# Attention scores in eight array tiles of one head each, with the previous half group's weighing put into the right halves of the same four banks

## The chip, the cores and the metric

The kernel runs on one core of one Trainium2 chip. The time is that of the device for one execution, in microseconds (us). TensorE (PE) does matrix products into PSUM, VectorE (DVE) and ScalarE (ACT) read PSUM and do elementwise work, GpSimd (POOL) does elementwise work in SBUF only, SyncE (SP) issues the transfers. PSUM has eight banks of 128 partitions by 512 fp32 values.

## The reference

Four residual layers follow one another on 128 graphs of 64 nodes with 256 features: `x = x + layer(relu(layernorm(x)))`. Layers 0 and 1 are attention layers with eight heads of 32 features. Layer 0 masks by the adjacency; layer 1 adds the logarithm of the adjacency to the scores. The part that the change touches, cut to what matters:

```python
q = split_heads(x @ Wq + bq)          # layer 1 has no q, k, v biases
k = split_heads(x @ Wk + bk)
v = split_heads(x @ Wv + bv)
scores = jnp.einsum('bhqd,bhkd->bhqk', q, k) / sqrt(HD)      # HD = 32
scores = jnp.where(adj > 0, scores, NEG)                     # layer 0
scores = scores + jnp.log(adjacency + 1e-06)                 # layer 1
attn = softmax(scores, axis=-1)
out = jnp.einsum('bhqk,bhkd->bhqd', attn, v)                 # called weighing below
return out @ Wo + bo
```

Layer 2 is a gated recurrent unit over five rounds of `A.T @ (h @ weight[l])`; its gates make up most of the matrix work. Layer 3 is a gated pair of graph convolutions.

## The kernel before, in words

**Tiling and stages.** Two graphs make a pair of 128 rows, four pairs make a group, and there are 16 groups. Attention works on half a group at a time (two pairs), so there are 16 x 2 layers x 2 halves = 64 calls of `attend`, the half groups of this text. Everything is fp32; each fp32 matmul that isn't a transpose stands twice in the profile's records, as two passes.

**Order of the work.** The instructions are not issued in program order. Every operation is handed to a planner (class `Plan`) with its engine, an assumed cost, its reads and writes, and a due time. The stages lie on strands: the attention of group g+1 (`front`), the recurrent rounds of group g (`gru`) and layer 3 of an earlier group (`back`) overlap. The planner walks through time and writes one fixed order for each engine's queue. On the chip every engine then works through its queue in that order and waits where a semaphore is not yet there. The constants at the head (`AHEAD`, `FRONT_LAST`, `STEP_SPAN`, `LOCK` and so on) shift due times. `CHANGE` holds the costs that the planner assumes for a switch between the modes of the array: whole (`WIDE`), tiles of 64 rows by 64 columns (`T64`), tiles of 64 by 32 (`T32`), and transposes (`TURN`).

**PSUM.** Four of the eight banks (`gate`, tag "g") are kept for the gates of the recurrent unit: tiles `gb`, `gc`, `nb`, `nc`, line 994. The other four (`bank`, tag "a") serve everything else: layernorm transposes `lnT` (L547), `qkvb` and `qkvc` (L711), scores `s`, weighing `o`, output projection `y` (L879), aggregation `agg` (L1034), transposes `hT`, and layer 3 (`l3b`, `l3c`, `hom`).

**Attention of one half group.** `by_seven` (58 of the 64) or `plainly` (6) make q, k and v. `spread` (L653, ACT) then copies k twice into `k_exp`: one copy keeps the even heads and zeroes the odd ones, the other the reverse. With it one score matmul covers 64 rows of q (two heads) and yields both heads side by side: 16 matmuls of 64 x 64 weights and 128 moving columns (L775), on four tiles of the array, into two banks. ACT takes the exponential of each bank (L797, two instructions of 512 columns), and POOL multiplies by the mask (L799). Weighing is done one half group later: `weigh` (L843, and L851 for the sums of the exponentials by a column of ones) in tiles of 64 by 32 into two further banks, where the left half of a bank holds outputs and the right half sums. `divide` on DVE turns the sums (L861), takes the reciprocal (L862), turns it back (L863) and multiplies (L865) into `oT`. Four matmuls of `y` and the residual addition (L882) end it. Weighing of the last half group and scores of this one are two separate operations of the planner, so that other work may stand between them.

A second copy of the whole network (`lean` false) stands behind a branch that is not taken here.

Of the kernel before, what the change touches and what calls it, by code (L numbers as in the profile page):

```python
# [55 lines left out]
AHEAD = 2.0  # L56
# [4 lines left out]
FRONT_LAST = 0.15  # L61
# [3 lines left out]
BACK_SPAN = 0.7  # L65
STEP = 0.0
STEP_LAST = -0.1
STEP_SPAN = 0.5
LOCK = 0.3
BACK_END = 0.1  # L70
ENTRY = 0.05
FIRST = -1.2
# [6 lines left out]
WEIGH = (655, 950)  # L79
MASK_UP = 2.0 ** 32  # L80
# [208 lines left out]
def network(ctx: ExitStack, tc: tile.TileContext, a: dict, out: bass.AP, flag):  # L289
# [343 lines left out]
    def attend(layer, xt, half, bias, bias_at, name, plain):  # L633
# [7 lines left out]
        k_exp = new("kexp", [P, 2, 2, HALF], 1, f"kexp_{name}")  # L641
# [17 lines left out]
        def plainly():  # L659

            (tq, jq), (tk, jk), (tv, jv) = of_first[layer]

            def dense(ps, t, j, hold):
                for o in range(2):
                    for kc in range(2):
                        pe(mm(256), lambda o=o, kc=kc: nc.tensor.matmul(
                            ps[:, o * HALF : (o + 1) * HALF], t[:, j, kc, o * P : (o + 1) * P], hT[:, kc, :],
                            start=kc == 0, stop=kc == 1), [(t, j), hT], [ps], holds=[hold])

            pq, pk, pv = bank(f"q_{name}"), bank(f"k_{name}"), bank(f"v_{name}")  # L670
            split = lambda ps: ps.tile.rearrange("p (c g t) -> p c g t", c=2, g=2)
            dense(pq, tq, jq, qk)
            if biased:
                for c in range(2):
                    vec(dve(256, 1), lambda c=c: nc.vector.tensor_scalar(
                        qk[:, c, :, 0, :], split(pq)[:, c], cols[:, c : c + 1], None, op0=ALU.add),
                        [pq, cols], [(qk, (c, 0))])
            else:
                vec(dve(512), lambda: nc.vector.tensor_copy(qk[:, :, :, 0, :], split(pq)), [pq], [(qk, (0, 0))])
            dense(pk, tk, jk, k_exp)  # L680
            spread(lambda c: split(pk)[:, c], [pk])
            for gp in range(2):
                for kc in range(2):
                    pe(mm(256), lambda gp=gp, kc=kc: nc.tensor.matmul(
                        pv[:, gp * D : (gp + 1) * D], side(kc, gp)(), tv[:, jv, kc, :],
                        start=kc == 0, stop=kc == 1), [(tv, jv), hT], [pv], holds=[v])
            sca(act(512), lambda: nc.scalar.activation(
                v.tile, pv.tile.rearrange("p (g f) -> p g f", g=2), AF.Copy), [pv], [v])

        def by_seven():  # L690
# [27 lines left out]
            def keep(bk, nm, c):  # L718

                t = new("cp", [P, 4, P], 5, f"{nm}_{name}")  # L720
                if biased:
                    sca(act(128, 1), lambda: nc.scalar.activation(
                        t[:, 0, :], bk[:, :P], AF.Identity, bias=cols[:, c : c + 1]), [bk, cols], [(t, 0)])
                    sca(act(256), lambda: nc.scalar.activation(t[:, 1:3, :], part(bk, 1), AF.Copy), [bk], [(t, 1)])
                else:
                    sca(act(384), lambda: nc.scalar.activation(t[:, :3, :], part(bk), AF.Copy), [bk], [(t, 0), (t, 1)])
                return t

            def total(bk, t, c, gp):
                vec(dve(256), lambda: nc.vector.tensor_tensor(  # L730
                    qk[:, c, gp], part(bk, 0, 2), t[:, :2, :], op=ALU.add), [bk, (t, 0), (t, 1)], [(qk, (c, gp))])
# [16 lines left out]
            if biased:  # L748
                for j in range(2):
                    sca(act(128, 1 - j), lambda j=j: nc.scalar.activation(  # L750
                        qk[:, 1, 0, j, :], pb[:, j * P : (j + 1) * P], AF.Copy if j else AF.Identity,
                        **({} if j else dict(bias=cols[:, 1:2]))), [pb, cols], [(qk, (1, 0, j))])
            else:
                sca(act(256), lambda: nc.scalar.activation(qk[:, 1, 0], part(pb, 0, 2), AF.Copy), [pb], [(qk, (1, 0))])
            sca(act(128), lambda: nc.scalar.activation(v[:, 0, P:], pb[:, 2 * P : 3 * P], AF.Copy), [pb], [(v, (1, 0))])
            spread(lambda c: qk[:, c, :, 1, :], [qk])
# [6 lines left out]
        pss = [bank(f"s_{name}_{i}") for i in range(2)]  # L763

        def scores():
            for outer in range(2):
                for c in range(2):
                    for inner in range(2):
                        for rh in range(2):
                            i, gp = (inner, outer) if lean else (outer, inner)  # L770
# [3 lines left out]
                            to, at = (i, gp) if lean else (gp, i)  # L774
                            nc.tensor.matmul(ps[to * NODES : (to + 1) * NODES, 2 * c : 2 * c + 2, at, :],  # L775
# [5 lines left out]
        if waiting:  # L781
# [12 lines left out]
        for i in range(2):  # L794
            ps, e = pss[i], es[i]
            if lean:
                sca(act(512, 0.5), lambda ps=ps, e=e: nc.scalar.activation(  # L797
                    e.tile, ps.tile.rearrange("p (h k) -> p h k", h=4), AF.Exp, scale=scale), [ps], [e])
# [3 lines left out]
                continue  # L802
# [30 lines left out]
        po = [bank(f"o_{name}_{i}") for i in range(2)]  # L833

        def weigh():
            for gp in range(2):
                s = slice(gp * NODES, (gp + 1) * NODES)
                for c in range(2):
                    for q in range(4):
                        for i in range(2):  # L840
                            rows, h = slice(i * NODES, (i + 1) * NODES), 4 * c + q
                            o = po[i][:, :D].rearrange("p (c t) -> p c t", c=2)
# [5 lines left out]
                for q in range(4):  # L848
                    for i in range(2):
                        rows = slice(i * NODES, (i + 1) * NODES)  # L850
                        nc.tensor.matmul(po[i][q * HD : (q + 1) * HD, D:], ones[rows, :],  # L851
# [3 lines left out]
        oT = new("oT", [P, 2, 2, P], 1, f"oT_{name}")  # L855

        def divide(i):
            zt = new("zt", [P, D], 2, f"zt_{name}_{i}")
            rz = new("rz", [P, HEADS], 2, f"rz_{name}_{i}")
            blocks = lambda t: t.tile.rearrange("p (b t) -> p b t", t=32)  # L860
            vec(dve(256), lambda: nc.vector.transpose(zt.tile, po[i][:, D:]), [po[i]], [zt])  # L861
            vec(109, lambda: nc.vector.reciprocal(rz[:, :, None], blocks(zt)[:, :, :1]), [zt], [rz])  # L862
            vec(dve(256), lambda: nc.vector.transpose(  # L863
                blocks(zt), rz[:, :, None].to_broadcast([P, HEADS, 32])), [rz], [zt])
            vec(dve(256), lambda: nc.vector.scalar_tensor_tensor(  # L865
                oT[:, i].rearrange("p c t -> p (c t)"), zt.tile, WEIGH_UP, po[i][:, :D],
                op0=ALU.mult, op1=ALU.mult), [po[i], zt], [(oT, i)])

        def finish():
            for i in range(2):  # L870
                if lean:
                    divide(i)
                    continue
                vec(dve(256), lambda i=i: nc.vector.tensor_copy(
                    oT[:, i], po[i][:, :D].rearrange("p (c t) -> p c t", c=2)), [po[i]], [(oT, i)])
            py = bank(f"y_{name}")
            for i in range(2):
# [7 lines left out]
                [py, (xt, pp), (xt, pp + 1)], [(xt, pp), (xt, pp + 1)])  # L885

        waiting.append((xt, weigh, [v, *aTs], po, oT, finish))

    def flush(xt):

        if not waiting or waiting[-1][0] is not xt:
            return
        _, weigh, reads, po, oT, finish = waiting.pop()
        pe(WEIGH[lean], weigh, reads, po, holds=[oT], mode=T32)
        finish()
# [638 lines left out]
```

## Time and profile before

| | |
|---|---|
| time, median of 3 (lowest to highest) | 2507.91 us (2506.99 to 2508.75) |
| span of the profiled execution | 2505.0 us |
| PE busy | 2483.1 us, 99% |
| DVE busy | 1875.7 us, 75% |
| ACT busy | 1304.8 us, 52% |
| POOL busy | 889.4 us, 36% |
| score matmuls (L775), records | 2048, 69.7 us busy |
| weighing matmuls (L843 and L851), records | 4096 and 1024, 71.8 and 49.8 us busy |
| copies into k_exp (L653) | 192, 98.2 and 10.2 us busy |
| exponentials (L797) | 128, 69.5 us busy |

Busy time of matmuls on array tiles overlaps, so a burst's real cost is read from the timeline: from its first start to the start of what follows. The rows of a group give the mean duration of one instruction and, behind the bar, how long its engine was idle just before it.

### The profile page before, as it was taken

The numbers are of one execution on the slowest core, as the hardware profiler recorded it, in microseconds if no ns is written. First come the engines' busy times: TensorE is split into PE (matmuls) and PEld (weight loads), VectorE is DVE, ScalarE is ACT, GpSimd is POOL, SyncE is SP. The second block draws the span as 40 slices with busy tenths as digits, with TensorE's granted clock in tenths as the row PEclk, the third lists the DMA queues.
The fourth block names the chain that finished last, engine by engine and source line by source line (L and its number), as shares of the span: only waits on it lengthen the run. The fifth ranks groups of instructions, "written<-read, shape, count | busy, mean of one in ns | idle before, by whom it ended". The sixth has DMA issues, their size and how long they took to land.

```text
span 2505.0 us, 58714 instructions
## 1 busy us (share of the span) xinstructions
PE 2483.1 (99%) x24057; PEld 2131.6 (85%) x24057; DVE 1875.7 (75%) x4396; ACT 1304.8 (52%) x2654; POOL 889.4 (36%) x894
## 2 busy tenths in 40 slices
PE   9999999999999999999999999999999999999997
PEld 7888888888888888888888888888888888888885
DVE  6666777777777777787778777777777777877667
ACT  3455454555555455555554555555554555555544
POOL 6633433333333332423334333333333424333221
PEclk9999999999999999999999999999999999999999
DMA  6411212112222121222113122122221212211120
GB/s 207 171 61 64 94 62 88 65 53 84 72 80 72 62 74 65 82 69 80 59 62 102 50 88 83 52 81 72 80 68 59 76 66 80 72 46 71 49 71 19
DMA packets 78266, 188.60 MB, mean 75 GB/s; under 512 B 14802, under 2 KB 66852, under 8 KB 67108
## 3 DMA queue, kind: packets, MB, share of 16 engines
q1 hardware_dynamic: 77872, 184.71, 21.6%
q8 instruction: 192, 3.15, 0.5%
q14 instruction: 86, 0.70, 0.1%
q10 hardware_dynamic: 116, 0.04, 0.0%
HBM read 166.70 MB, written 18.02 MB: 74 GB/s over the span
## 4 chain that ended last, share of the span: by engine, by line
PE 97%; DVE 2%; ACT 0%; issue 0%; POOL 0%; DMA 0%; DVEq 0%; ACTq 0%; POOLq 0%
PE gb L994 22%; PE gc L994 17%; PE nb L994 11%; PE nc L994 8%; PE qkvb L711 6%; PE qkvc L711 5%; PE y L879 4%; PE agg L1034 3%; PE l3b L1339 3%; PE s L775 2%; PE l3c L1339 2%; PE lnT L547 2%; PE hT L547 2%; PE o L843 2%; PE o L851 1%; PE gv L930 1%
## 5 line engine op out<-in xcount | busy, mean ns | idle before, releaser
L1103 POOL TENSOR_TENSOR sn<-h,sn 128x512 f32<-128x512 f32 x158 | 205.5, 1304 | 664.3 <-ACT sn L1101 664.3
L994 PE MATMUL gb<-Ta,gv 128*128 128x256 f32 x960 | 248.1, 381 | 0.0
L994 PE MATMUL gb<-Th,w_hh 128*128 128x256 f32 x960 | 247.9, 381 | 0.0
L963 POOL TENSOR_TENSOR Th<-h 128x256 f32<-128x256 f32 x160 | 120.4, 772 | 333.6 <-PE nb L994 230.6
L533 POOL TENSOR_TENSOR rstd<-pw,few 128x2 f32<-128x2 f32 x128 | 94.9, 741 | 382.6 <-DVE pw L532 380.6
L799 POOL TENSOR_TENSOR e<-e,mask 128x512 f32<-128x512 f32 x128 | 176.2, 1396 | 105.9 <-ACT e L797 105.9
L994 PEld LDWEIGHTS gb<-Th,w_hh 128*128 128x128 f32 x960 | 177.5, 190 | 23.4 <-issue 1.9
L994 PEld LDWEIGHTS gb<-Ta,gv 128*128 128x128 f32 x960 | 177.1, 191 | 23.4 <-issue 2.1
L1101 ACT ACTIVATE sn<-sn,b_n 128x512 f32<-128x512 f32 x158 | 113.4, 722 | 132.9 <-DVE sn L1099 132.5
L994 PE MATMUL gc<-h,w_hh 128*128 128x256 f32 x640 | 167.4, 384 | 0.1
L994 PE MATMUL gc<-agg,gv 128*128 128x256 f32 x640 | 164.6, 380 | 0.0
L1105 DVE SCALAR_TENSOR_TENSOR sn<-sg,sn 128x512 f32<-128x512 f32 x158 | 107.4, 686 | 62.9 <-POOL sn L1103 62.6
L1086 ACT ACTIVATE sg<-sg,b_rz 128x512 f32<-128x512 f32 x158 | 106.6, 715 | 90.3 <-DVE sg L1066 90.2
L963 POOL TENSOR_TENSOR Th<-h,Th 128x256 f32<-128x256 f32 x160 | 144.8, 905 | 8.6 <-DVE h L1107 2.9
L1097 DVE SCALAR_TENSOR_TENSOR sn<-sg,sn 128x512 f32<-128x512 f32 x158 | 118.6, 758 | 37.1 <-ACT sn L1208 30.5
L994 PE MATMUL nb<-Th,w_hh 128*128 128x256 f32 x480 | 144.5, 383 | 0.1
L994 PE MATMUL nb<-Ta,gv 128*128 128x256 f32 x480 | 144.3, 382 | 0.0
L994 PEld LDWEIGHTS gc<-h,w_hh 128*128 128x128 f32 x640 | 117.0, 190 | 23.4 <-issue 2.5
L879 PE MATMUL y<-w_L_gnn_Wo,oT 128*128 128x256 f32 x512 | 135.6, 380 | 0.1
L994 PEld LDWEIGHTS gc<-agg,gv 128*128 128x128 f32 x640 | 120.7, 190 | 16.0 <-issue 0.2
L1047 DVE TENSOR_TENSOR Ta<-agg 128x256 f32<-128x256 f32 x160 | 88.7, 574 | 50.8 <-PE nb L994 33.0
L1107 DVE SCALAR_TENSOR_TENSOR h<-sn 128x512 f32<-128x512 f32 x158 | 122.2, 780 | 5.6 <-ACT e L797 0.5
(228 smaller groups left out, 6527.2 us busy)
## 6 DMA issues: line engine op xcount, KB each, us to landing
gv<-gates SPq DMA_DIRECT2D x80, 1344.0 KB, 5.9
qw<-kept SPq DMA_DIRECT2D x203, 192.0 KB, 2.5
x<-in_x_dram SPq DMA_DIRECT2D x32, 256.0 KB, 3.4
out_dram<-x SPq DMA_DIRECT2D x32, 256.0 KB, 2.9
gates<-gv SPq DMA_DIRECT2D x5, 1344.0 KB, 4.9
adjq<-in_adj_dram SPq DMA_DIRECT2D x8, 256.0 KB, 5.2
gw<-in_L_gnn_weight_dram SPq DMA_DIRECT2D x5, 256.0 KB, 6.4
kept<-s SPq DMA_DIRECT2D x8, 128.0 KB, 3.4
```

What stands on the lines that cost most here:

```text
L711: nc.tensor.matmul(bk[:, j * P : (j + 1) * P], lhs, rhs, start=first and j == 0, stop=True, skip_group_check=True)
L799: pool(1000, lambda e=e: nc.gpsimd.tensor_tensor(e.tile, e.tile, bias_at(pp)[:, None, :].to_broadcast([P, 4, 2 * NODES]), op=ALU.mult), [e ...
L879: pe(mm(256), lambda i=i, c=c: nc.tensor.matmul(py[:, i * D : (i + 1) * D], oT[:, i, c, :], w_o[:, c, :], start=c == 0, stop=c == 1), [(oT ...
L963: pool(690, lambda: nc.gpsimd.tensor_tensor(T[:, i, :], x(), y(), op=ALU.subtract), reads, [(T, i)])
L994: nc.tensor.matmul(bank_[:, col * HALF : (col + 1) * HALF], at(g, n), rhs(), start=first and j == 0, stop=True, skip_group_check=True)
L1086: sca(act(TOK, 1.5), lambda k=k, col=col: nc.scalar.activation(g_v[:, :, k, :], g_v[:, :, k, :], AF.Tanh, bias=b_rz[:, col : col + 1], sca ...
L1097: vec2(dve(TOK), lambda: nc.vector.scalar_tensor_tensor(a_(), r(), 1.0, a_(), op0=ALU.add, op1=ALU.mult), [*ts[0], n_v], [n_v])
L1101: sca(act(TOK, 1.5), lambda: nc.scalar.activation(a_(), a_(), AF.Tanh, bias=b_n[:, oc : oc + 1]), [n_v, b_n], [n_v])
L1103: pool(1230, lambda: nc.gpsimd.tensor_tensor(b_(), hh(), a_(), op=ALU.subtract), [*hp, n_v], [n_v])
L1105: vec2(dve(TOK), lambda: nc.vector.scalar_tensor_tensor(b_(), z(), 1.0, b_(), op0=ALU.add, op1=ALU.mult), [*ts[1], n_v], [n_v])
L1107: vec2(dve(TOK), lambda: nc.vector.scalar_tensor_tensor(hh(), b_(), 0.5, a_(), op0=ALU.mult, op1=ALU.add), [n_v], hp)
L1339: pe(mm(384), lambda: nc.tensor.matmul(bk[:, : 3 * P], b(), w3[:, :, n, :], start=first, stop=True, skip_group_check=True), [w3, *reads], ...
```

## The change

In the `lean` network `k_exp` and `spread` go. k is written beside q in `qk`, with its bias where there is one. The scores are now 32 matmuls for a half group with 32 rows (one head), 64 x 64 out, on eight tiles of 32 rows by 64 columns: row block r of the array writes to bank r, so that a half group takes four banks, of which it fills the left halves. In the right halves of the same four banks stands the weighing of the previous half group: outputs in banks 0 and 2, sums in banks 1 and 3. Weighing and scores are one planner operation (`burst`), so they always stand next to each other. It starts when all four "a" banks are free. The exponentials become four of 256 columns each (banks 0, 2, then 1, 3). `divide` becomes a generator: all turns and reciprocals first, then the exponentials are queued, then the two multiplications. ACT and DVE never read one bank at once: each of these reads is entered as a write. The planner's constants are set anew.

It is meant to halve the columns that pass through the array for the scores, to use the array's eight tiles, and to do without the copies of k. The diff, cut to its core:

```diff
-AHEAD = 2.0
+AHEAD = 1.85
-FRONT_LAST = 0.15
+FRONT_LAST = 0.25
-BACK_SPAN = 0.7
+BACK_SPAN = 0.8
-STEP_LAST = -0.1
-STEP_SPAN = 0.5
-LOCK = 0.3
-BACK_END = 0.1
-ENTRY = 0.05
-FIRST = -1.2
+STEP_LAST = -0.25
+STEP_SPAN = 0.4
+LOCK = 0.4
+BACK_END = 0.0
+ENTRY = -0.05
+FIRST = -1.15
+SCORES = 600
...
-            spread(lambda c: split(pk)[:, c], [pk])
+            if not lean:
+                spread(lambda c: split(pk)[:, c], [pk])
+            elif biased:
+                for c in range(2):
+                    sca(act(256, 1), lambda c=c: nc.scalar.activation(
+                        qk[:, c, :, 1, :], split(pk)[:, c], AF.Identity, bias=cols[:, 2 + c : 3 + c]),
+                        [pk, cols], [(qk, (c, 1))])
+            else:
+                sca(act(512), lambda: nc.scalar.activation(qk[:, :, :, 1, :], split(pk), AF.Copy), [pk], [(qk, (0, 1))])
...
-                if biased:
+                if biased and lean:
+                    for j in range(2):
+                        sca(act(128, 1), lambda j=j: nc.scalar.activation(
+                            t[:, j, :], bk[:, j * P : (j + 1) * P], AF.Identity,
+                            bias=cols[:, 2 * j + c : 2 * j + c + 1]), [bk, cols], [(t, ("j", j))])
+                    sca(act(128), lambda: nc.scalar.activation(t[:, 2:3, :], part(bk, 2), AF.Copy), [bk], [(t, 1)])
+                elif biased:
...
-        pss = [bank(f"s_{name}_{i}") for i in range(2)]
+        pss = [bank(f"s_{name}_{i}") for i in range(4 if lean else 2)]
 
         def scores():
+            for part in range(4) if lean else ():
+                c, gp = divmod(part, 2)
+                for r in range(4):
+                    for i in range(2):
+                        s = slice(r * HD, (r + 1) * HD)
+                        n = slice(i * NODES, (i + 1) * NODES)
+                        nc.tensor.matmul(pss[r][n, part * NODES : (part + 1) * NODES],
+                                         qk[s, c, gp, 0, n], qk[s, c, gp, 1, n], start=True, stop=True)
+            if lean:
+                return
...
+        if lean:
+            beside = [(pss[2 * i + z], D) for i in range(2) for z in range(2)]
+            last = waiting.pop() if waiting else None
+
+            def burst():
+                if last:
+                    last[1](beside)
+                scores()
+
+            pe(WEIGH[True] + 135 + SCORES if last else SCORES, burst, [qk, *(last[2] if last else [])], pss,
+               holds=[*es, *([last[4]] if last else [])], mode=T32 if last else T64, leaves=T64)
+            if last:
+                finish_last = last[5](beside)
+                next(finish_last)
...
-                sca(act(512, 0.5), lambda ps=ps, e=e: nc.scalar.activation(
-                    e.tile, ps.tile.rearrange("p (h k) -> p h k", h=4), AF.Exp, scale=scale), [ps], [e])
+            for r in (0, 2, 1, 3):
+                sca(act(256, 0.5), lambda r=r: nc.scalar.activation(
+                    es[r // 2].tile.rearrange("p (c r) t -> p r c t", r=2)[:, r % 2],
+                    pss[r][:, :D].rearrange("p (c t) -> p c t", c=2), AF.Exp, scale=scale), [], [pss[r], (es[r // 2], r)])
+                if r == 2 and finish_last:
+                    for _ in finish_last:
+                        pass
...
+                ps, lo = at[2 * i + 1]
+                vec(dve(256), lambda zt=zt, ps=ps, lo=lo: nc.vector.transpose(zt.tile, ps[:, lo : lo + D]), [], [ps, zt])
+                vec(109, lambda rz=rz, blocks=blocks: nc.vector.reciprocal(rz[:, :, None], blocks()[:, :, :1]), [zt], [rz])
+                vec(dve(256), lambda rz=rz, blocks=blocks: nc.vector.transpose(
+                    blocks(), rz[:, :, None].to_broadcast([P, HEADS, 32])), [rz], [zt])
+            yield
+            for i in range(2):
+                ps, lo = at[2 * i]
+                vec(dve(256), lambda i=i, zt=zts[i], ps=ps, lo=lo: nc.vector.scalar_tensor_tensor(
+                    oT[:, i].rearrange("p c t -> p (c t)"), zt.tile, WEIGH_UP, ps[:, lo : lo + D],
+                    op0=ALU.mult, op1=ALU.mult), [zts[i]], [ps, (oT, i)])
```

Places to find in the changed kernel: scores L789, exponentials L837, weighing L890 and sums L899, the steps of `divide` L911 to L918, `y` L932, gates L1065.

## The prediction

> **What bounds the kernel now.** I read the stretches of time first, then the chain that ended last, then TensorE's timeline around the score bursts, and last the timeline of all engines around one burst.
>
> ```profile
> 200.00:2237.00 2037.00, 2036.03 (x20172) 1762.13 (x20174) 1550.78 (x3661) 1084.87 (x2223) 715.12 (x700) 1.00 0.21 71
> 2237.00:2505.00 268.00, 250.76 (x1848) 205.98 (x1837) 191.58 (x395) 129.69 (x250) 69.20 (x73) 0.99 0.15 55
> ...
> PE 97%; DVE 2%; ACT 0%; issue 0%; POOL 0%; DMA 0%; DVEq 0%; ACTq 0%; POOLq 0%
> ```
>
> The columns after the length are busy time of PE, weight loads, DVE, ACT and POOL. Between 200 us and the end of attention at 2237 us PE lacks 1.0 us of the whole 2037; the last chain is 97% PE. So the time is the sum of what stands in PE's queue, and one microsecond taken out of that queue is one microsecond of the result, as long as no new wait appears. DVE (76% there) and ACT (53%) only matter where PE waits for them. The clock is full.
>
> ```profile
> 619.62 0.59 PE L994 MATMUL nc<-Ta,gv 128*128 128x256 f32 x2
> 620.05 0.59 PE L994 MATMUL nb<-Th,w_hh 128*128 128x256 f32 x2
> 620.57 0.45 PE L843 MATMUL o<-e,v 64*32 64x64 f32 x32
> 620.84 0.78 PE L851 MATMUL o<-e,ones 64*32 64x256 f32 x16
> 621.27 0.66 PE L843 MATMUL o<-e,v 64*32 64x64 f32 x32
> 621.86 1.10 PE L775 MATMUL s<-kexp,qk 64*64 64x128 f32 x32
> 622.89 0.70 PE L994 MATMUL nb<-Ta,gv 128*128 128x256 f32 x2
> 623.43 1.03 PE L994 MATMUL gc<-h,w_hh 128*128 128x256 f32 x4
> ```
>
> From starts alone: weighing takes 621.86 - 620.57 = 1.29 us, scores 622.89 - 621.86 = 1.03. The plain pair before is 0.43 apart from its follower (620.05 - 619.62); the pair ahead of the burst 0.52, the one behind it 0.54. Going into tiles therefore costs 0.09 and the first whole-array pair afterwards 0.11. The single records of the score burst come in eight rounds of four tiles, 0.109 apart; 8 x 0.109 = 0.87, so that 0.16 of the 1.03 is the way out.
>
> ```profile
> 1002.36 1.16 PE L1034 MATMUL agg<-A,ht 64*64 64x64 f32 x64
> 1003.34 1.06 PE L775 MATMUL s<-kexp,qk 64*64 64x128 f32 x32
> 1004.33 0.92 PE L994 MATMUL gb<-Th,w_hh 128*128 128x256 f32 x3
> ```
>
> Aggregation and scores use the same 64 x 64 tiles. Ahead of scores it takes 0.98; ahead of whole-array work 1.09 in the other places. A shared mode thus saves 0.11.
>
> **What the Trainium skill says.** (1) "TensorEngine Tiling (Array Packing)", Tiling Modes: 32 x 64 gives eight tiles, 64 x 64 four, and changing the mode drains the engine. The 0.16, 0.11 and 0.09 above agree with a drain; no 32 x 64 burst is in this trace. (2) The same page, Restrictions and Gotchas: different row tiles may not write one bank at once, so four row blocks need four banks. The trace has two row blocks with two banks, which fits. (3) "TensorE: Matmul & The Clock Gate", Part 3: matmuls of different tiles overlap, and weight loads run ahead where the row group differs. The weighing (eight tiles of 64 x 32) agrees: its first 32 records take 0.27 us, while aggregation's 64 on four tiles take 0.98. (4) "PSUM — Partial Sum Buffer", on bank collisions: two engines may not be in one bank and quadrant together. Hence exponentials and the turns of the sums now take turns on banks 1 and 3; before they had banks of their own, so no row shows that wait.
>
> **The change part by part.**
>
> *Scores.* A half group has 64 records of 64 columns instead of 32 of 128. Nearest row: 32 records of that width on eight tiles in 0.27 us (620.57 to 620.84). Its rounds of eight lie 0.055 apart, after a first of 0.08. Eight rounds give 8 x 0.055 + 0.03 = 0.47, twice the row 0.54. With 0.16 for the way out: 0.63 to 0.70. The worst bound is that eight tiles bring nothing over four: then 64 records cost what aggregation's 64 cost, 1.09. I take 0.65, because the weighing already shows eight tiles fed at full rate and a half-size step in the pace would have no cause in this trace. Saving 1.03 - 0.65 = 0.38, times 64 half groups: 24.3 us off PE's queue. At 0.76 it would be 17 us, at 1.09 a loss of 4.
>
> *Weighing* keeps its matmuls, in the same order and tile mode; only banks differ. Zero.
>
> *Switches.* Before, I count in the timeline 139 stretches of tile work: 29 weighing+scores, 22 aggregation+scores, 4 scores+aggregation, 14 aggregation+weighing, 40, 21 and 9 alone of aggregation, weighing and scores. The order of instructions as built for the changed kernel has 145: 61 weighing+scores, 1 with aggregation ahead of these, 79 aggregations, 2 weighings and 2 scores alone. So fusing doesn't lessen them: scores lose aggregation as a neighbour. 6 more stretches at 0.09 + 0.11 = 1.2 us, and 26 shared modes lost at 0.11 = 2.9. Sum +4.1.
>
> *Four banks at once.* What is behind the burst in PE's queue is gate work, which has its own four banks. Here is what frees the "a" banks:
>
> ```profile
> 926.31 1.10 PE L775 MATMUL s<-kexp,qk 64*64 64x128 f32 x32
> 926.40 0.78 DVE L861 STREAM_TRANSPOSE zt<-o 128x256 f32<-128x256 f32 x2 [2.55 <-PE o L843]
> 927.11 0.32 DVE L862 RECIPROCAL rz<-zt 128x8 f32<-128x8 f32 x2
> 927.34 0.74 DVE L863 STREAM_TRANSPOSE zt<-rz 128x256 f32<-128x256 f32 x2
> 927.47 1.08 ACT L797 ACTIVATE e<-s 128x512 f32<-128x512 f32 x2 [1.74 <-PE s L775]
> 928.00 0.71 DVE L865 SCALAR_TENSOR_TENSOR oT<-zt,o 128x256 f32<-128x256 f32 x2
> ```
>
> DVE starts 0.24 after the last weighing matmul starts (median of the 64) and has the first `oT` 2.08 later. Now the turns read banks that scores write as well, so I count them from the end of the scores: `y` can start 0.24 + 2.08 + 0.2 = 2.5 after the last score matmul, or 2.35 after the next whole-array matmul. Exponentials start 0.32 after the last score matmul; four of 256 columns (about 0.28 apart, half of 0.49 plus a fixed part) with banks 1 and 3 behind the turns free bank 1 at about 1.65. In the built order the first use of an "a" bank stands mostly 1.3 or 1.73 us of gate work behind the burst, `y` 2.16 to 2.6, and the third use beyond 4.1 in nearly all. The margins are thus from -0.2 to +0.3 us. Some 30 bursts wait 0.1: +3 us. Both ends: 0, if turns and exponentials start early enough everywhere, and 0.4 x 62 = 25 us, if DVE's queue is each time one or two 0.4 us instructions late.
>
> *ACT.* 192 copies go (98.2 + 10.2 us); 10 copies of k out of PSUM (5), 128 more exponentials (256 x 0.38 - 69.5 = 28) and a third, biased piece in 84 copies of layer 0 (84 x 0.26 = 22) come: about -53 us, from 1305 to 1250. PE waits for none of it between 200 and 2237 us, so it is worth nothing there; POOL's mask multiplication and the next weighing lie some 39 us (2505/64) apart.
>
> *The constants* put the last group's rounds elsewhere. PE idles 17 us in the last stretch and 4 in the first 200 us. I take 0, with 3 us either way.
>
> Sum: 2507.9 - 24.3 + 4.1 + 3 = **2491 us**.
>
> **The rivals.**
> (B) *Eight tiles, but slower rounds* (0.76 a burst, for example because four row blocks load 64-column weights: those loads take 133 ns in the score rows, 107 in the weighing's). 2507.9 - 17 + 4 + 4 = 2499. For it: no row shows four row blocks at once. Against: the weighing's pace.
> (C) *No gain from eight tiles* (1.09): 2507.9 + 4 + 4 + 3 = 2519, slower. Against it, again, the weighing.
> (D) *The lock on four banks becomes the bound*: PE waits 0.4 per burst, 2507.9 - 24 + 4 + 25 = 2513, slower. For it: DVE is busy 76%, its turns now begin about 0.65 us later against the following `y`, and the burst itself must wait for four free banks. Against: the order has gate work at these places, and in the kernel before, where 29 bursts also hold four banks, PE lost 1.0 us in 2037.
>
> **How the numbers follow.** Forecast 0.62, B 0.16, D 0.14, C 0.08. B counts as faster, C as slower; of D some half is smaller waits that land within 0.2% (5 us) of before. Faster 0.77, same 0.07, slower 0.16. Range: down to 2483 (0.63 a burst, no waits, the ends 3 us better: 2507.9 - 25.6 + 4.1 - 3 = 2483); up to 2508, which takes in B and the milder half of D and leaves out C and the rest of D.
>
> **What would show it.** Right: the score burst 0.63 to 0.70 from its start to the next whole-array matmul; PE still 99% busy, with under 5 us of idle between 200 us and the end of attention; weighing 1.29; ACT near 1250 us. Wrong: a pace of the score records near 0.015 us (C) or a first round much longer; PE idle ahead of `y`, `lnT` or the burst, with DVE's turns or an exponential as the releaser (D); a weighing longer than 1.29 because its sums go to other banks; or a last stretch much beyond 268 us, which would be the constants.

## The result, and the profile after

| | before | after |
|---|---|---|
| time, median (lowest to highest) | 2508.33 us (2506.99 to 2508.91, 4 runs) | 2517.98 us (2514.57 to 2519.54, 4 runs) |
| ratio to before | | 1.0037 [1.002, 1.0055] |
| span of the profiled execution | 2505.0 us | 2512.8 us |

The change makes the kernel slower by 9.7 us. The prediction was 2491 us with 0.16 for slower; it was wrong.

The stretches of the changed kernel (length, then busy time of PE, weight loads, DVE, ACT and POOL) and its chain that ended last:

```profile
200.00:2237.00 2037.00, 2029.58 (x21718) 1756.40 (x21718) 1537.99 (x3652) 1031.87 (x2237) 733.64 (x703) 1.00 0.21 71
2237.00:2512.00 275.00, 256.85 (x1971) 209.65 (x1969) 195.02 (x400) 132.90 (x259) 69.52 (x73) 0.99 0.15 53
```

```profile
PE 94%; DVE 4%; ACT 1%; issue 1%; DMA 0%; POOL 0%; DVEq 0%; ACTq 0%; POOLq 0%
```

Where PE lacked 1.0 us of 2037 before, it now lacks 2037 - 2029.58 = 7.4, and DVE has 4% of the chain instead of 2%. What PE waits for is in the view of its waits (total, times, longest); first the changed kernel, then the one before:

```profile
PE lnT L548 <- DVE xn L578: 8.4, 13, 0.9
PE gb L1065 <- ACT agg L1111: 2.9, 3, 1.2
PE wT L990 <- ACT e L837: 1.4, 2, 1.0
...
PE s L890 <- ACT agg L1111: 0.5, 1, 0.5
PE s L890 <- ACT v L771: 0.5, 1, 0.5
```

```profile
PE lnT L547 <- DVE xn L577: 2.2, 3, 1.2
PE gb L994 <- ACT agg L1040: 1.2, 1, 1.2
```

New in size is the wait of the transpose of layernorm (`lnT`) for `xn`, the normalized rows that DVE makes for it. No score burst, `y` or weighing is in this list with an exponential or a turn as its releaser. Two transposes of weights (`wT`) wait for exponentials and two weighings for copies by ACT, all within the first 200 us.

Now one burst of the changed kernel in the timeline (start, length from first start to last end, engine, line; "x" counts records), and the work behind it:

```profile
1082.67 0.45 PE L890 MATMUL s<-e,v 64*32 64x64 f32 x32
1082.94 0.78 PE L899 MATMUL s<-e,ones 64*32 64x256 f32 x16
1083.37 0.66 PE L890 MATMUL s<-e,v 64*32 64x64 f32 x32
1083.96 0.91 PE L789 MATMUL s<-qk 32*64 32x64 f32 x64
1084.80 1.13 PE L1065 MATMUL gb<-Th,w_hh 128*128 128x256 f32 x4
...
1085.96 0.66 ACT L837 ACTIVATE e<-s 128x256 f32<-128x256 f32 x2
...
1086.64 0.71 DVE L918 SCALAR_TENSOR_TENSOR oT<-zt,s 128x256 f32<-128x256 f32 x2
...
1087.34 1.46 DVE L578 TENSOR_SCALAR xn<-x,mv,rstd 128x256 f32<-128x256 f32 x1
1087.39 2.54 POOL L844 TENSOR_TENSOR e<-e,mask 128x512 f32<-128x512 f32 x2
1087.50 1.89 PE L932 MATMUL y<-w_L_gnn_Wo,oT 128*128 128x256 f32 x8
1088.73 0.68 DVE L1137 TENSOR_TENSOR sg<-gb,p5g 128x512 f32<-128x512 f32 x1
1089.23 0.27 PE L548 MATMUL lnT<-ident,xn 128*128 128x128 f32 x1
1089.33 0.75 DVE L578 TENSOR_SCALAR xn<-x,mv,rstd 128x256 f32<-128x256 f32 x1
1090.14 0.55 PE L548 MATMUL lnT<-ident,xn 128*128 128x128 f32 x3 [0.64 <-DVE xn L578]
```

Two things are to be seen. First, weighing takes 1083.96 - 1082.67 = 1.29 us, as before, but the scores 1084.80 - 1083.96 = 0.84, where 0.65 was predicted. Over all 62 joint bursts the median is 2.130 us for both; 1.288 + 1.034 = 2.322 before. So a burst saves 0.19, not 0.38. Inside the scores every eighth record starts 0, 107, 165, 223, 292, 458, 538 and 604 ns after the first, the last at 696. After the first eight, the first 32 come at some 58 ns for eight, near the pace that the prediction took for all 64. The other 32 need 101 ns for eight on average, 1.7 times that.

Second, the instruction `xn` takes 0.41 us (its median) in most places, but here 1.46 and 0.75, and both times the mask multiplication of the exponentials runs on POOL. Both end 0.15 us after one of the two multiplications ends. This is no accident: in all 13 traces of this study, 345 instructions `xn` took over 0.6 us, and each of them ended 0.15 to 0.16 us after the end of a POOL instruction. The gate sum `sg` and the second `xn` stand behind it in DVE's queue, and so `lnT` comes 0.64 late. Meanwhile `y` ran without a wait. The same picture returns every 153 us, once for each group, 11 times between 477 and 2007 us.

The kernel before has such a place 11 times too, with 1.05 us for one `xn` and the usual time for the next, but there `lnT` comes late enough not to wait:

```profile
1118.11 2.50 POOL L799 TENSOR_TENSOR e<-e,mask 128x512 f32<-128x512 f32 x2
1119.71 1.38 DVE L577 TENSOR_SCALAR xn<-x,mv,rstd 128x256 f32<-128x256 f32 x2
1121.42 0.60 PE L547 MATMUL lnT<-ident,xn 128*128 128x128 f32 x4
```

Summing the time from each record's start to the next start gives the balance of the two profiled runs, in us (that of the changed kernel is the fastest of its four, 2514.57):

| what stood on PE | before | after | difference |
|---|---|---|---|
| weighing and scores | 147.6 | 140.5 | -7.1 |
| aggregation | 86.3 | 88.8 | +2.5 |
| transposes, with the waits behind them | 152.8 | 161.5 | +8.7 |
| whole-array matmuls, with the waits behind them | 2098.3 | 2101.5 | +3.2 |
| sum | 2485.0 | 2492.3 | +7.3 |

The -7.1 holds 3.7 us by which some of the 62 joint bursts are longer than the median; without them it would be -10.8. Some 3.0 of the 3.7 are in four bursts of the first 200 us, most of it the waits for ACT in the list above: behind one burst `wT` waits for an exponential, and in two the weighing waits.

### The profile page after: what moved, and what is told of

The parts are those of the page before. It is cut to its first block, busy times and chain, and to the rows that moved or that the text cites. A ratio compares the mean times of both kernels' runs of the same rounds, so it can differ in the third digit from the quotient of the medians.

```text
span 2512.8 us, 63087 instructions
## 1 busy us (share of the span) xinstructions
PE 2480.9 (99%) x26105; PEld 2128.7 (85%) x26105; DVE 1864.7 (74%) x4396; ACT 1246.1 (50%) x2684; POOL 907.5 (36%) x894
## 4 chain that ended last, share of the span: by engine, by line
PE 94%; DVE 4%; ACT 1%; issue 1%; DMA 0%; POOL 0%; DVEq 0%; ACTq 0%; POOLq 0%
PE gb L1065 21%; PE gc L1065 17%; PE nb L1065 11%; PE nc L1065 8%; PE qkvb L720 6%; PE qkvc L720 5%; PE y L932 4%; PE agg L1105 3%; PE l3b L1410 3%; PE l3c L1410 2%; PE hT L548 2%; PE s L789 2%; PE lnT L548 2%; PE s L890 2%; PE s L899 1%; PE gv L1001 1%
## 5 line engine op out<-in xcount | busy, mean ns | idle before, releaser
L534 POOL TENSOR_TENSOR rstd<-pw,few 128x2 f32<-128x2 f32 x128 | 107.3, 839 | 473.2 <-DVE pw L533 472.1
L1065 PE MATMUL gb<-Th,w_hh 128*128 128x256 f32 x960 | 249.2, 382 | 0.0
L1065 PE MATMUL gb<-Ta,gv 128*128 128x256 f32 x960 | 248.2, 381 | 0.0
L1034 POOL TENSOR_TENSOR Th<-h 128x256 f32<-128x256 f32 x160 | 137.1, 877 | 270.2 <-PE nb L1065 168.3
L844 POOL TENSOR_TENSOR e<-e,mask 128x512 f32<-128x512 f32 x128 | 170.6, 1354 | 138.6 <-ACT e L837 138.6
L1065 PEld LDWEIGHTS gb<-Th,w_hh 128*128 128x128 f32 x960 | 179.1, 190 | 29.3 <-issue 2.1
L1065 PEld LDWEIGHTS gb<-Ta,gv 128*128 128x128 f32 x960 | 178.3, 191 | 22.9 <-issue 0.4
L1065 PE MATMUL gc<-agg,gv 128*128 128x256 f32 x640 | 165.6, 382 | 0.0
L1065 PE MATMUL gc<-h,w_hh 128*128 128x256 f32 x640 | 165.2, 381 | 0.1
L1176 DVE SCALAR_TENSOR_TENSOR sn<-sg,sn 128x512 f32<-128x512 f32 x158 | 116.9, 740 | 43.6 <-POOL sn L1174 43.5
L1168 DVE SCALAR_TENSOR_TENSOR sn<-sg,sn 128x512 f32<-128x512 f32 x158 | 118.4, 749 | 37.6 <-ACT sn L1279 33.4
L1137 DVE TENSOR_TENSOR sg<-gc,ug 128x512 f32<-128x512 f32 x80 | 54.7, 683 | 120.9 <-PE gc L1065 120.7
L1065 PE MATMUL nb<-Th,w_hh 128*128 128x256 f32 x480 | 143.2, 380 | 0.0
L1065 PE MATMUL nb<-Ta,gv 128*128 128x256 f32 x480 | 143.2, 380 | 0.0
L1065 PEld LDWEIGHTS gc<-h,w_hh 128*128 128x128 f32 x640 | 118.9, 190 | 20.5 <-ACT sn L1279 4.2
L1065 PEld LDWEIGHTS gc<-agg,gv 128*128 128x128 f32 x640 | 120.5, 190 | 16.4
L837 ACT ACTIVATE e<-s 128x256 f32<-128x256 f32 x256 | 81.6, 384 | 102.1 <-PE s L789 101.5
L932 PE MATMUL y<-w_L_gnn_Wo,oT 128*128 128x256 f32 x512 | 126.3, 380 | 0.0
```

Of the source, the lines that this page charges most:

```text
L534: pool(660 if n == 2 else 970, lambda: nc.gpsimd.tensor_tensor(dst.tile, s.tile, few[:, 1 : 1 + n], op=ALU.pow), [s, (few, 1)], [dst], port=2)
L844: pool(1000, lambda e=e: nc.gpsimd.tensor_tensor(e.tile, e.tile, bias_at(pp)[:, None, :].to_broadcast([P, 4, 2 * NODES]), op=ALU.mult), [e ...
L932: pe(mm(256), lambda i=i, c=c: nc.tensor.matmul(py[:, i * D : (i + 1) * D], oT[:, i, c, :], w_o[:, c, :], start=c == 0, stop=c == 1), [(oT ...
L1034: pool(690, lambda: nc.gpsimd.tensor_tensor(T[:, i, :], x(), y(), op=ALU.subtract), reads, [(T, i)])
L1065: nc.tensor.matmul(bank_[:, col * HALF : (col + 1) * HALF], at(g, n), rhs(), start=first and j == 0, stop=True, skip_group_check=True)
L1168: vec2(dve(TOK), lambda: nc.vector.scalar_tensor_tensor(a_(), r(), 1.0, a_(), op0=ALU.add, op1=ALU.mult), [*ts[0], n_v], [n_v])
```

## The experiments

The order of all queues comes from the planner's assumed costs. A change of constants or costs therefore gives another order, while an edit inside one operation leaves the order as it is. Both kinds are among the runs, and only the second isolates one cost.

**The constants.** One run gives the changed kernel the nine old constants, one gives the kernel before the nine new ones.

```diff
-AHEAD = 1.85
+AHEAD = 2.0
...
-LOCK = 0.4
+LOCK = 0.3
...
-FIRST = -1.15
+FIRST = -1.2
```

> The changed kernel with the nine planner constants of before. Theory A (the new constants are at fault: they were set for a burst that costs less than it does, and a better order exists with the old ones): faster than the changed kernel, 2500 to 2510 us. Theory B (the new constants are what keeps the waits small with four banks locked; the loss has other causes): slower than the changed kernel, over 2525 us, with more idle time on TensorE between 200 us and the end of attention than the changed kernel's 7.4 us.

> The kernel before with the nine constants of the changed kernel. If the constants by themselves cost the 10 us: about 2518 us. If they fit the changed code alone: clearly over 2520 us. If they are neutral: 2505 to 2511 us.

Measured: 2519.62 us (2518.12 to 2520.10), ratio to before 1.0047 [1.0033, 1.0061], which is neither of the two expectations but the time of the changed kernel; and 2567.57 us (2566.24 to 2569.95), 1.0239 [1.0225, 1.0253], for the kernel before with the new constants, 60 us more. So going back to the old constants doesn't take the loss away, and the new ones don't suit the code before. With the old constants the loss of the changed kernel stands in other places: `lnT` waits for `xn` only 2.7 us, but the joint bursts are 8.8 us over their median and aggregation takes 91.2 us instead of 86.3. The step "constants 0, with 3 us either way" holds for the changed code.

**Twice the scores, same order.**

```diff
-                for r in range(4):
+                for r in (0, 1, 2, 3, 0, 1, 2, 3):
```

> The changed kernel with every score matmul issued twice into the same place, the planner's costs unchanged. 64 more records in each of 64 half groups. Theory supply (records after the first 32 of a burst arrive about 17 ns apart, because that is the pace at which TensorE's queue hands out pairs of weight load and matmul): 64 x 0.0167 = 1.07 us a burst, +68 us, about 2586 us. Theory array (eight tiles run a round in 0.055 us, and what made the score burst 0.84 instead of 0.65 us is a fixed cost of the new tile mode): 8 x 0.055 = 0.44 us a burst, +28 us, about 2546 us.

Measured: 2632.67 us (2622.0 to 2637.36), 1.049 [1.0467, 1.0514]. A burst without a pause took 1.523 us instead of 0.843: 64 further pairs of weight load and matmul cost 0.68, 10.6 ns each, between the 0.44 and the 1.07 of the theories; the time lies above both. Beyond the first 32, then, a pair costs 10.6 ns and not 7. 64 x 0.68 = 43.5 of the 115 us are that; most of the rest are pauses inside the bursts:

```profile
PE s L789 <- issue: 44.4, 34, 3.4
```

"issue" means that the profile shows nothing for which PE waits. By the starts of the records there are 38 pauses of over 0.17 us inside bursts, 54 us together. Of these, 36 (52.5 us) ended 1.3 to 1.6 us after a packet of 16 KB on the instruction queue had ended; the other two, 0.7 us each, are the weighings that wait for ACT in the changed kernel as well. The granted clock of the profiled run was 0.990, against 0.998 in the changed kernel, and part of the remaining 19 us may lie there. This is that queue in the kernel before, the changed one and the one with twice the scores (packets, MB, share):

```profile
q8 instruction: 192, 3.15, 0.5%
```

```profile
q8 instruction: 208, 3.41, 0.6%
```

```profile
q8 instruction: 240, 3.93, 0.6%
```

From run to run 16 packets come with 2048 further pairs and 32 with 4096, so a packet is 256 instructions of TensorE. More instructions are thus fetched. That PE runs out of them in dense bursts fits, but the fetch itself wasn't changed in any run, so its part rests on this coincidence in time. In the changed kernel it is small: of five pauses of over 0.17 us inside its bursts, three, 0.75 us together, end 1.4 to 1.5 us after such a packet, and the other two are the waits for ACT.

**Half the instructions, same columns, same order.** The scores of the second half of the queries are left out (they get those of the first half), and 16 matmuls with 128 moving columns stand for 32 with 64.

```diff
-                for r in range(4):
+                for r in range(4) if not gp else ():
...
-                        nc.tensor.matmul(pss[r][n, part * NODES : (part + 1) * NODES],
-                                         qk[s, c, gp, 0, n], qk[s, c, gp, 1, n], start=True, stop=True)
+                        nc.tensor.matmul(pss[r][n, c * P : (c + 1) * P],
+                                         qk[s, c, 0, 0, n], qk[s, c, :, 1, n], start=True, stop=True)
```

> The changed kernel in its own order, but each half group's scores are 16 pairs of weight load and matmul with 128 moving columns (on the eight tiles, two per tile) instead of 32 pairs with 64. The columns through the array stay as they are (2 x 2 x 128 against 4 x 2 x 64 a tile, with both passes), the instructions halve. It leaves out the scores of half of the queries: the second half gets the first half's q, so that the output is not the reference's. Instruction supply (the first 32 pairs run at the eight tiles' pace because they already wait in the queue, later ones come at 10.6 ns each): the burst shrinks from 0.84 to about 0.65 us, 0.19 x 64 = 12 us less on TensorE, total 2504 to 2508. Array theory (the eight tiles simply need 0.84 for these columns, or the first weights of four row blocks cost it): the burst stays 0.80 to 0.85 us, total 2515 to 2519.

Measured: 2507.59 us (2505.92 to 2509.49, 13 runs), 0.9998 [0.999, 1.0007]. Its timeline around one burst:

```profile
865.00 0.69 PE L789 MATMUL s<-qk 32*64 32x128 f32 x32
865.62 1.13 PE L1065 MATMUL gc<-agg,gv 128*128 128x256 f32 x4
```

The burst takes 0.62 us with the same columns on the same eight tiles and four row blocks. This settles the size of the burst: the array can do it in the predicted time, and the number of pairs is what costs 0.22 us. Bursts fell by 14.7 us in the balance of the trace (140.5 to 125.8), but whole-array work with its waits grew by 5.3 and transposes by 2.2; `lnT` waits 9.3 us here. So one microsecond taken out of PE's queue no longer is one microsecond of the result: with a burst as short as predicted, the time is still 17 us above 2491. No pause of this run follows an instruction packet (its queue has 192, as before), and yet its joint bursts are 3.1 us over their median; so most of the 3.7 in the changed kernel isn't due to the number of instructions.

**The mask multiplication almost gone, same order.** It covers 32 of the 512 columns; 15/16 of the masking is left out.

```diff
-                    e.tile, e.tile, bias_at(pp)[:, None, :].to_broadcast([P, 4, 2 * NODES]), op=ALU.mult),
+                    e[:, :, :8], e[:, :, :8], bias_at(pp)[:, None, :8].to_broadcast([P, 4, 8]), op=ALU.mult),
```

> The changed kernel with GpSimd's multiplication of the exponentials by the mask cut from 512 to 32 columns an instruction; this leaves out 15/16 of the masking. The order of all queues is as in the changed kernel. Theory port (in each group VectorE's xn is held 1 us by this multiplication, and the transposes lnT then wait 0.8 us, 13 times): xn keeps to 0.41 us there, TensorE's waits on xn fall from 8.4 us to under 2 us, the time to about 2508 us. Theory queue (VectorE's chain of turns and reciprocals is late by itself): lnT still waits, time over 2514 us.

> The kernel before with the same cut of the mask multiplication to 32 columns (15/16 of the masking left out). Theory port-after (the hold of VectorE by GpSimd's mask multiplication costs time only in the order of the changed kernel): 2505 to 2508 us, since TensorE lacks just 1.0 us between 200 and 2237 us. Rival (the multiplication costs both kernels alike, so it doesn't explain their difference): about 2493 us, as far below before as the same cut brought the changed kernel down (15 us).

Measured: 2503.23 us (2501.5 to 2505.24, 21 runs), 0.9981 [0.9975, 0.9988], on the changed kernel, 14.7 us less than that; on the kernel before 2503.41 us (2502.58 to 2505.17, 21 runs), 0.9985 [0.9978, 0.9991], about 4 less (the ratio gives 3.8). This lies between the two expectations, nearer to the first. The difference, some 11 us by the medians and 8 by the profiled spans, is what the multiplication costs the changed kernel more than the old one; without it the two are equal. The place shown above, in the changed kernel with the small mask, and its stretch:

```profile
1083.76 0.44 DVE L578 TENSOR_SCALAR xn<-x,mv,rstd 128x256 f32<-128x256 f32 x1
1083.81 0.51 POOL L844 TENSOR_TENSOR e<-e,mask 128x32 f32<-128x32 f32 x2
1083.92 1.89 PE L932 MATMUL y<-w_L_gnn_Wo,oT 128*128 128x256 f32 x8
1084.73 0.40 DVE L578 TENSOR_SCALAR xn<-x,mv,rstd 128x256 f32<-128x256 f32 x1
1085.43 0.57 PEld L548 LDWEIGHTS lnT<-ident,xn 128*128 128x128 f32 x4
```

```profile
200.00:2237.00 2037.00, 2035.25 (x21834) 1767.39 (x21832) 1506.02 (x3666) 1037.92 (x2255) 629.24 (x708) 1.00 0.21 72
```

The order of the instructions is the same, `xn` takes 0.44 and 0.40, the four transposes run together, and PE lacks 1.75 us instead of 7.4. The groups of `xn` in the changed kernel and in this one (busy, mean ns):

```profile
L578 DVE TENSOR_SCALAR xn<-x,mv,rstd 128x256 f32<-128x256 f32 x192 | 97.5, 537 | 20.6 <-POOL rstd L534 17.4 <-PE lnT L548 2.4 <-ACT ht L582 0.7
```

```profile
L578 DVE TENSOR_SCALAR xn<-x,mv,rstd 128x256 f32<-128x256 f32 x192 | 80.8, 450 | 21.0 <-POOL rstd L534 17.0 <-PE lnT L548 3.1 <-ACT ht L582 0.7
```

**The mask multiplication in two pieces, same order**, nothing left out.

```diff
-                pool(1000, lambda e=e: nc.gpsimd.tensor_tensor(
-                    e.tile, e.tile, bias_at(pp)[:, None, :].to_broadcast([P, 4, 2 * NODES]), op=ALU.mult),
-                    [e, bias], [e])
+                pool(1000, lambda e=e: [nc.gpsimd.tensor_tensor(
+                    e[:, h : h + 2, :], e[:, h : h + 2, :], bias_at(pp)[:, None, :].to_broadcast([P, 2, 2 * NODES]),
+                    op=ALU.mult) for h in (0, 2)], [e, bias], [e])
```

> The changed kernel in its own order with its computation complete; each mask multiplication is issued as two GpSimd instructions of 256 columns inside one planner operation. Theory of the held port (VectorE's xn waits until the running GpSimd instruction lets go): the longest hold is halved, so of the roughly 8 us that lnT waits for xn some half goes: total 2511 to 2515, and the waits of lnT for xn 3 to 5 us. Rival (GpSimd's whole time in that stretch counts, whatever its pieces, or shorter pieces only cost a fixed part more): same within 2 us of the changed kernel, 2516 to 2520, waits of lnT still near 8 us.

Measured: 2516.49 us (2515.96 to 2518.28), 1.0036 [1.0022, 1.0049]. The waits did what the held port says, the time what its rival says:

```profile
PE lnT L548 <- DVE xn L578: 4.2, 13, 0.9
PE gb L1065 <- ACT agg L1111: 2.9, 3, 1.2
PE s L789 <- issue: 1.6, 4, 0.7
```

At the 11 places `xn` now takes 0.92 and 0.90 us instead of 1.46 and 0.75, one short piece being its hold each time, and `lnT` waits half as long. Long joint bursts grew from 3.7 to 5.7 us over the median: five pauses, 2.7 us, now follow an instruction packet, instead of three with 0.75. Whole-array work grew by 3.4. Why these grew in the same order stays open. As a remedy it fails.

**Fusing alone.** The kernel before, with its old scores, but weighing and scores as one operation that needs all four banks.

```diff
-            pe(WEIGH[lean], weigh_last, reads, po_last, holds=[oT_last], mode=T32)
-            pe(860, scores, [qk, k_exp], pss, holds=es, mode=T64)
+            pe(WEIGH[True] + 30 + 860, lambda: (weigh_last(), scores()), [*reads, qk, k_exp], [*po_last, *pss],
+               holds=[oT_last, *es], mode=T32, leaves=T64)
```

> The kernel before with one part of the change alone: weighing and scores are one operation of the planner that needs all four banks at once; scores keep k_exp, four tiles and their two banks, the constants are those of before. Theory fuse (holding four banks at once and losing aggregation as a neighbour in the same tile mode is the larger part of the loss): slower by the 4 us of the lost neighbours and by new waits, 2514 to 2525 us. Rival (fusing is harmless, the loss is in what the eight tiles and the half banks bring): 2505 to 2512 us.

Measured: 2554.38 us (2552.85 to 2555.95), 1.0187 [1.0173, 1.0201], far from every expectation. PE lacks 21.5 us between 200 and 2237 us and waits 15.3 us for the copies of aggregation; what follows 2237 us lasts 317 us, 49 longer than before. The planner with the old constants makes a bad order of the fused operation, so this run says nothing on the worth of fusing.

**Costs nearer to the measured ones, constants set anew.** Two runs of the changed code (both with weighing assumed at 1.15 and scores at 0.70 us instead of 0.95 and 0.60, but other constants), and one of the code before with weighing at 1.15.

```diff
-WEIGH = (655, 950)
-SCORES = 600
+WEIGH = (655, 1150)
+SCORES = 700
```

> The changed kernel with the planner's costs of weighing and scores set to what the traces show (1150 and 700 instead of 950 and 600) and the due-time constants set anew for them. Theory cost (the recurring wait of lnT comes from an order made for a burst that ends 0.3 us too early): TensorE's waits on xn under 2 us, idle between 200 us and the end of attention under 4 us, 2500 to 2508 us. Rival (with four banks locked any order has such waits): 2512 us or more.

> The kernel before with the planner's cost of weighing set to 1150 and the due-time constants set anew. TensorE lacks 1.0 us in the middle stretch already, so it can gain at the two ends alone: 2500 to 2509 us. Should e7 gain on the changed kernel and this one not on before, the costs are a fault of the change's order; should both gain alike, it is the constants' search that gains.

> The changed kernel with the burst's costs in the planner set near the measured ones (weighing 1.15, scores 0.70) and its other constants set anew together, so that only the order differs. If the change is worth its 12 us of shorter bursts once the order keeps xn clear of GpSimd, 2500 to 2508, with PE idle below 4 us between 200 and 2237 us. If each order brings its own waits and the changed code has no more slack to give, 2515 to 2530.

Measured: 2523.47 us (2521.39 to 2526.44), 1.0069 [1.0055, 1.0083], the first order of the changed code: `lnT` waits only 1.3 us for `xn`, but whole-array work with its waits takes 13 us more than in the changed kernel, so wrong costs alone weren't the cause. The other order of the changed code: 2507.56 us (2505.86 to 2509.08, 13 runs), 0.9998 [0.9989, 1.0006]; PE lacks 6.0 us between 200 and 2237 us, where under 4 was expected. The code before: 2504.11 us (2502.36 to 2505.55, 21 runs), 0.9986 [0.9979, 0.9992], the fastest complete kernel of the study.

The waits of PE in the better order of the changed code:

```profile
PE s L789 <- issue: 4.3, 4, 1.7
PE f L1381 <- ACT hT L553: 2.2, 2, 1.1
PE gv L1001 <- issue: 1.6, 1, 1.6
```

No wait of `lnT` for `xn` is left between 200 and 2237 us. Its four pauses in bursts (0.4 to 1.9 us, 5.2 together) all end 1.25 to 1.45 us after an instruction packet. Weighing and scores take 142.9 us, aggregation 87.3, transposes 152.7: 4.7 us won in the bursts against the kernel before, 5.4 lost again in aggregation and in whole-array work with its waits. This best order of the changed code only reaches the time of before.

## Why the prediction was wrong, point by point

*PE is the bound.* Right as a reading of the kernel before. The clause "one microsecond taken out of that queue is one microsecond of the result, as long as no new wait appears" lost its condition: with half the score instructions, 14.7 us left the bursts and 7.5 came back in longer transposes and whole-array stretches, waits included.

*Scores: 0.65 us instead of 1.03, 24.3 us saved.* This term was mis-sized: 0.84, and 64 x 0.19 = 12 us. I took the pace of the weighing's first 32 records for 64 of them, and wrote that a slower pace "would have no cause in this trace". The cause was the number of records, and the lines that I showed had a sign of it: the weighing's last 32 records, of the same shape on the same tiles, take 621.86 - 621.27 = 0.59 us, or 0.43 without the 0.16 for the way out, where the first 32 take 0.27. In the scores the first 32 pairs come at 7 ns each after the first eight, further ones at 10.6. The Trainium skill ("TensorE: Matmul & The Clock Gate", Part 1, on engine queue depths) gives TensorE a queue of 64 instructions; 32 pairs of load and matmul are 64. The break after 32 pairs agrees with this, and halving the instructions shows that their number matters, not the tiles; no run changed the queue itself. The step of rival B (0.76) was thus nearer in size, but for another cause than it gave. A second part was missing: long bursts take 3.7 us off the 10.8, mostly by waits for ACT in the first 200 us; pauses that follow an instruction packet are some 0.8 of it.

*Weighing: zero.* Right, 1.29.

*Switches: +4.1.* Right in kind and about right in size. Aggregation, which lost the neighbour with its mode, costs +2.5; the lost neighbour on the side of the scores is inside the -10.8 (12 less some 1).

*Four banks at once: +3.* The size of the waits failed, and the place too. I counted margins for the "a" banks and `y`. These held: `y` follows without a wait at 1087.50. The wait came where I had put no cost, at `xn`. For the place, the timeline above: exponentials and both `oT` end between 1086.6 and 1087.35, and right after that both POOL's multiplication and DVE's next instruction begin, which in this order is `xn`. The Trainium skill ("SBUF — State Buffer", SBUF: two separate sides) says that VectorE in some modes and GpSimd hold a port pair exclusively, for a whole instruction. The traces agree: 1.46 us with a multiplication of 1.27 ahead, 0.92 with one of 0.73, 0.44 with a small one, and each long `xn` ends 0.15 us after a POOL instruction; in which mode `xn` runs, no run shows. The small mask shows the price, some 8 to 11 us more than in the kernel before, which has the hold too but at a place where PE doesn't wait for it. Which of the change's parts brings `xn` to that place is not separated: the old constants leave the time as it is, with other losses, and another set removes the wait from the same code. It belongs to the built order, then, and not to the bursts.

*ACT near 1250 us, worth nothing.* Right: 1246.1 us, and no gain from it.

*Constants: 0 +-3.* Right for the two sets that came with the kernels, on the changed code. It understated what an order is worth: the changed code took 2507.6 to 2523.5 us in four orders, a spread of 16 us, more than the 12 us by which the shorter bursts could shorten PE's queue.

*Rivals.* The time is near D's 2513 (slower), but D's cause is hardly there: no `y` waits behind DVE's turns, and of waits around the bursts there are only the four of the list above, 2.4 us together. What it did name rightly is DVE as the engine that PE comes to wait for. C (1.09 a burst) falls with the 0.84.

The sum with the measured terms, from the balance: -10.8 in unpaused bursts, +3.7 longer bursts, +2.5 aggregation, +8.7 at transposes (mostly `lnT` for `xn`), +3.2 at whole-array work = +7.3 us between the two profiled runs, whose spans differ by 7.8. The prediction's sum was -17.2. Of the 24.5 us between, the bursts make up 16.0 (-24.3 + 1.2 forecast, -7.1 measured), and transposes and whole-array work with their waits 8.9 (+3 forecast, 8.7 + 3.2 measured); aggregation is 0.4 better than the 2.9 forecast. The size of the score burst, 12 of the 16.0, is thus the larger miss, and the waits, above all that of `lnT` for `xn`, are the second.

## What to carry to other kernels

A pace read from a short burst holds for bursts of that many instructions: count pairs of load and matmul, not only columns, before extending it, and prefer fewer matmuls with more columns where both fill the same tiles. When an edit moves exponentials or DVE work, look up what DVE does while POOL runs; a wait for an `xn` that takes 1.46 us instead of 0.41 shows in no margin of banks. Where a planner fixes the order, compare the two codes each in an order set for it, and test costs with edits that leave the order alone.

## What the hardware showed that I had not expected

- After the first 32 pairs of the score burst on eight tiles, each further pair of weight load and matmul costs 10.6 ns (0.68 us for 64), against 7 ns within the first 32; 32 pairs with 128 columns on the same eight tiles take 0.62 us, 64 pairs with 64 columns 0.84.
- TensorE pauses of up to 3.6 us inside dense bursts, each ending 1.3 to 1.6 us after a 16 KB packet on the instruction queue: 1 pause in the kernel before, 3 (0.75 us) in the changed one, 36 (52.5 us) with twice the scores. That the packet is what they wait for isn't shown.
- A DVE instruction of 0.41 us is stretched to 1.46 by a POOL multiplication of 1.27 that runs beside it, though both only touch SBUF; beside pieces of 0.73 us it takes 0.92. In 13 traces all 345 `xn` of over 0.6 us end 0.15 to 0.16 us after a POOL instruction.
